# Attention phase of a two-layer gated cross-attention kernel: the weight combinations move from GpSimd to VectorE, three groups of instructions get other places

## The chip, the cores and the metric

The kernel runs on one NeuronCore of a Trainium2 chip. TensorE (PE) multiplies and transposes, VectorE (DVE) and ScalarE (ACT) empty its PSUM banks and do the elementwise work, GpSimd (POOL) does some elementwise work on SBUF, and SyncE (SP) issues most transfers. The metric is the device time of one execution in microseconds. Before the change it is 2092.7 us, the median of three runs (2090.93 to 2093.04).

## The reference

The input x has 8 batches of 512 tokens with 512 features; each batch has a context of 64 tokens. Four residual blocks follow one another, each on a layernorm of x and with a tanh gate:

```python
# 1: linear attention over the context, 16 heads of 32
q = feature_map(xn @ Wq.T); gate = sigmoid(xn @ Wg.T + bg)
k, v = split(ctx @ Wkv.T);  k = feature_map(k)          # feature_map(x) = x+1 if x>0 else exp(x)
attn = (q @ (k.T @ v)) / (q . sum(k) + 1e-6)            # per head
x = x + tanh(g0) * ((attn * gate) @ Wo.T)
# 2: MLP 512 -> 2048 -> 512 with exact gelu
x = x + tanh(h0) * (gelu(xn @ p1.T + b1) @ p2.T + b2)
# 3: masked softmax attention over the context, no weights
x = x + tanh(g1) * softmax(mask(xn @ ctx.T / sqrt(512))) @ ctx
# 4: mixture of 8 dominant experts (router softmax, top 8 of 32, shares merged per group)
x = x + tanh(h1) * sum_g share_g * (silu(xn @ gate_g) * (xn @ up_g)) @ down_g
```

Everything is float32.

## The kernel before, in words

**Phases.** The batches go through three phases, each over all eight: "xa0" (block 1), "ff0" (block 2) and "ff1" (blocks 3 and 4). Between phases x lies in DRAM. Every large matrix product is done with seven instead of eight half-size products (Strassen's scheme in Winograd's form): the operands are first combined by additions. For activations VectorE does this per batch (`token_combinations`, tile S; `combine_inner`, tiles a and s). For weights it is done once per weight.

**Weights of ff0.** p1 and p2 must be combined before ff0 and stored to DRAM again. The generator `build_first` does so in the background of the attention phase, in four rounds i. A round loads a piece of p1 into seven ring tiles (`raw_p1`), combines it with four 128x512 additions (`combining`), stores the seven (`store_up`); loads a piece of p2 into the one build tile (`raw_p2`), combines it with four 128x512 additions, stores three parts of it, combines it a second time with four 128x896 additions in place (`combining_again`), and stores the other parts. Each `yield` ends one call. In the attention loop `tick()` is called after every step of TensorE work and calls the builder at ticks 1 and 3 of each five. All these additions run on GpSimd (`nc.gpsimd`). A second builder, `build_second`, does the like for the weights of ff1 during ff0, on VectorE, through `in_place`.

**Order of the work.** The code is traced in program order, and a planner then orders each engine's queue by its own estimate of when operands are ready. `Ordered` lets the code pin an instruction behind the one traced before it on the same engine: while an engine's name is in the set `in_order`, each of its instructions is pinned; `here(...)` adds engines for a few lines. In the preamble all engines are pinned. In the attention loop SyncE and GpSimd stay pinned, the others not. Each engine then works off its queue strictly in order.

**The preamble.** `keys_values` makes keys, values and, per batch, the key-value products (tile pkv, two PSUM banks per pair of batches), from which VectorE and ScalarE take `summary` and `ksum` (`kept`). Meanwhile batch 0 is normalised and turned.

**The attention loop.** For each batch b there are units of seven products each: `QUp` (queries), `GUp` (gates) and `ODown` (output projection) of the batch before; the last two products of a unit are done after the first of the next. A unit's step n is one product, eight matmuls. Between them stand the denominators of batch b (`denominators`: four matmuls pd, an addition and two reciprocals on VectorE, tile z, a store `over`), the spreading of their values over the heads' partitions by four transfers (`spread`), the gating th = (th + 1) * spread (`gated`, four instructions), the numerators pn on TensorE, and the products a = th * pn (`attended`), which ODown reads. For the last batch there is no next batch's work to hide this behind: `den` is advanced in its own GUp unit from n > 4 on, and from step 4 of ODown of batch 6 on VectorE is pinned, with `gated` after steps 4 and 5.

**Normalisation ahead.** `normed` computes the statistics of the next batch (bn_stats, tile st), rstd on GpSimd, normalises (ScalarE in most of xa0) and transposes. It is advanced by `some(prep)` at given steps; for xa0 and b > 0 first at step 4 of QUp. Its statistics are pinned on VectorE for batch 0 and for later ff0 batches, not for xa0 with b > 0 (line 480).

**Fetches on GpSimd.** The context for block 3 (`c2`, `ctxT` in `cross_attention`), the router weights and the map of expert groups are fetched by GpSimd's queue; in the feed-forward phases GpSimd is not pinned.

Of the kernel before, what the change touches and what calls it, by code (L numbers as in the profile page):

```python
# [30 lines left out]
P = 128  # L31
B, S, D = 8, 512, 512
M = 64
# [35 lines left out]
def flamingo_kernel(  # L69
# [334 lines left out]
    def placed(ph, t):  # L404

        return [t[:, SPLIT_ORDER[ph].index(m)] for m in (1, 5, 2, 3, 6, 7, 4)]

    def build_first():

        def load_up(i):
            t = [ring(f"raw_up{i}_{q}") for q in range(7)]
            raw_p1(t, i)
            return t

        up = load_up(0)
        yield
        for i in range(4):
            for n, _ in enumerate(combining(nc.gpsimd, up)):  # L420
                if n == 2:
                    t = build_tile(f"ff0_down{i}")
                    raw_p2(placed("ff0", t), i)
                yield
            store_up("ff0", i, up)
            for _ in range(2):
                yield
            for n, _ in enumerate(combining(nc.gpsimd, placed("ff0", t))):
                if n % 2:
                    yield  # L430
            if i < 3:
                up = load_up(i + 1)
            yield from combining_again("ff0", i, t, nc.gpsimd, 2)
            yield
        streamed.add("ff0")

    def in_place(steps):

        while True:
            in_order.add("vector")  # L440
            more = next(steps, steps)
            in_order.discard("vector")
            if more is steps:
                return
            yield

    LAND, GAP = 10, 5

# [23 lines left out]
    def normed(ph, b, tag, normed_part=lambda t: None):  # L472

        xb = xs[ph, b]
        xnT = work.tile([P, NC, S], F32, tag="xnT", name=f"xnT_{tag}")
        mv = small.tile([P, NT, 2], F32, tag="mv", name=f"mv_{tag}")
        held = ph == "ff0" and b > 1
        by_scalar = ph == "xa0" and b > 0 or tag == "ff0_0"
        ahead = held or ph == "xa0" and b > 0
        with here(*(["vector"] if held or ph == "xa0" and b == 0 else [])):  # L480
            for t in range(NT):
                st = small.tile([P, 6], F32, tag="st", name=f"st_{tag}_{t}")
                nc.vector.bn_stats(st, xb[:, t, :])
                nc.vector.bn_aggr(mv[:, t, :], st)
        var = small.tile([P, NT], F32, tag="var", name=f"var_{tag}")
        nc.vector.tensor_scalar(var, mv[:, :, 1], LN_EPS, None, ALU.add)  # L486
        rstd = small.tile([P, NT], F32, tag="rstd", name=f"rstd_{tag}")
        if by_scalar:
            shift = small.tile([P, NT], F32, tag="nshift", name=f"nshift_{tag}")
            nc.vector.tensor_scalar(shift, mv[:, :, 0], -1.0, None, ALU.mult)  # L490
        nc.gpsimd.tensor_tensor(rstd, var, neg_half, ALU.pow)  # L491
        if by_scalar:
            nc.gpsimd.tensor_tensor(shift, shift, rstd, ALU.mult)
        if ph in ("xa0", "ff0") or tag.startswith("ff1"):
            yield
        if tag.startswith("ff1"):
            yield
        xn = {}

        def norm(t):  # L500
            xn[t] = work.tile([P, D], F32, tag="xn", name=f"xn_{tag}_{t}")
            with here(*(["vector", "scalar"] if ahead else [])):
                if by_scalar:
                    nc.scalar.activation(
                        xn[t], xb[:, t, :], AF.Identity, bias=shift[:, t : t + 1], scale=rstd[:, t : t + 1]
                    )
                else:
                    nc.vector.tensor_scalar(
                        xn[t], xb[:, t, :], mv[:, t, 0:1], rstd[:, t : t + 1], ALU.subtract, ALU.mult
                    )  # L510

        def turn(t):
            pt = psum(f"pt_{tag}_{t}").rearrange("p (c q) -> p c q", q=P)
            for c in range(NC):
                nc.tensor.transpose(pt[:, c, :], xn[t][:, ts(c, P)], ident)  # L515

            at = t % 2 * 2 + t // 2 if tag.startswith("ff1") else t
            nc.scalar.copy(xnT[:, :, ts(at, P)], pt)

        if ph == "xa0" and b == 0:  # L520
            norm(0)
            norm(1)
            yield
            for t in range(NT):
                turn(t)
                if t + 2 < NT:
                    norm(t + 2)
                yield
            return xnT
        if ahead:  # L530
            norm(0)
            yield
        for t in range(NT):
            if not ahead:
                norm(t)
            elif t + 1 < NT:
                norm(t + 1)
            turn(t)
            normed_part(t)
            yield  # L540
        return xnT
# [109 lines left out]
    def cross_attention(b):  # L651

        xb = xs["ff1", b]
        c2 = hpool.tile([P, D], F32, tag="ctx", name=f"ctxd_{b}", bufs=2)
        for h in range(2):
            nc.gpsimd.dma_start(out=c2[ts(h, M), :], in_=ctx_in[ts(b, M), :])
        maskf = small.tile([P, M], F32, tag="maskf", name=f"maskf_{b}")
        in_order.add("vector")
        nc.vector.tensor_copy(maskf, mask_sb[:, ts(b, M)])
# [4 lines left out]
        nc.vector.reduce_max(gate, maskf, AX.X)  # L664
        nc.vector.tensor_scalar(gate, gate, gate_xa1, None, ALU.mult)
        ctxT = hpool.tile([P, NC, M], F32, tag="ctxdT", name=f"ctxdT_{b}", bufs=2)
        nc.gpsimd.dma_start(out=ctxT, in_=turned[b])
        xnT = yield from normed("ff1", b, f"xa1_{b}")


# [532 lines left out]
    def spread(b):  # L1203

        rows = over[b].rearrange("(c h k) t -> c k h t", c=NC, k=8)
        over[b] = aunits.tile([P, NC, S], F32, tag="over", name=f"spread_{b}")
        for c in range(NC):
            nc.sync.dma_start(out=over[b][ts(c, HD)], in_=rows[c, 0].partition_broadcast(HD))

    def gated(b, th, half):  # L1210

# [15 lines left out]
                )  # L1227
        return pn

    def attended(b, th, pn):  # L1230

        if b < B - 1:
            a = aunits.tile([P, 2, 2, 2, H2], F32, tag="a", name=f"a_{b}")
        else:
            a = work.tile([P, NC, S], F32, tag="xnT", name=f"a_{b}").rearrange(
                "p (r c) (n t) -> p r c n t", c=2, n=2
            )
        for h in range(NC):
            nc.vector.tensor_tensor(
                a[:, :, h // 2, h % 2, :], halves(th[:, h, :]), halves(pn[h]), ALU.mult  # L1240
            )
        for k in ("s1", "s2"):
            inner["x" + k] = aunits.tile([P, 2, H2], F32, tag=k, name=f"{k}_xa0_{b}")
        for r in range(2):
            for c in range(2):
                inner[f"xa{r + 1}{c + 1}"] = a[:, r, c]
        combine_inner(slice(0, 2), "x")
# [92 lines left out]

    def tick():

        if next(ticks) % 5 in (1, 3):
            next(builder, None)

    for b in range(B):
# [19 lines left out]
        for n, (u, m) in enumerate(steps([g])):  # L1366
            u.step(m)
            in_order.discard("tensor")
            tick()
            if n == 1:  # L1370
                if b + 2 < B:
                    load_x("xa0", b + 2)
                elif b + 1 == B:
                    load_x("ff0", 1)
            if b == B - 1 and n > 4:
                next(den, None)
            if n == 3 or n > 3 and not done:
                some(prep)
# [7 lines left out]
            spread(b)  # L1386
            pn = numerators(b, q.q)
        for n, (u, m) in enumerate(steps([ODown(done[0])] if done else [])):
            if b == B - 1 and n == 4:
                in_order.add("vector")  # L1390
            u.step(m)
            in_order.discard("tensor")
            if b < B - 1:
                next(den, None)
                if n == 6:
                    spread(b)
            elif n in (4, 5):
                gated(b, g.th, n - 4)
            elif n == 6:
                attended(b, g.th, pn)  # L1400
            if n in ((0, 1, 3, 5) if b < B - 1 else (6,)):
                some(prep)
            tick()
        in_order.discard("vector")
        for _ in prep:
            pass
        done = b, q.q, g.th
# [65 lines left out]
        next(loads)  # L1473
    hpool = stack(tc.tile_pool(name="inner", bufs=1, reuse_waits="tile"))
    router_sb = hpool.tile([P, NC, E], F32, tag="router_w", name="router_sb")
    nc.gpsimd.dma_start(out=router_sb, in_=router.rearrange("(c p) e -> p c e", p=P))

    of_group = hpool.tile([P, G, E], F32, tag="of_group", name="of_group")
    mg_i = hpool.tile([P, E], I32, tag="mg_i", name="mg_i")
    nc.gpsimd.dma_start(out=mg_i, in_=mg.rearrange("e o -> o e").partition_broadcast(P))  # L1480
    mg_f = hpool.tile([P, E], F32, tag="mg_f", name="mg_f")

    def groups():
        nc.vector.tensor_copy(mg_f, mg_i)
# [12 lines left out]
    for u, m, n in plan:  # L1497
# [29 lines left out]
            next(builder, None)  # L1527
        if n + 1 == 3 * B:
            continue
        if n == B + 2 and k == 10:  # L1530
            groups()
        if k == 20 and n + 2 < 3 * B:
# [61 lines left out]
```

## Time and profile before

| | |
|---|---|
| Median of the runs | 2092.7 us |
| Profiled execution, own time | 2091.8 us |
| Its span | 2090.0 us |
| Instructions in it | 35123 |
| Preamble, to the first q product | 0 to 61.2 us |
| Attention loop, to the first ff0 product | 61.2 to 412.9 us |
| ff0 and ff1 | 412.9 to 2090.0 us |
| VectorE busy, 61.2 to 350.0 | 208.6 of 288.8 us |
| GpSimd busy, 61.2 to 350.0 | 82.7 of 288.8 us |
| DMA moved | 484.67 MB |

A row of the profile names the line of the kernel, the engine, the operation and the tiles, output first ("ksum<-pkv,heads"). Line 60 is the wrapper `Ordered`: it stands for every pinned instruction, so those are told apart by tile. "xN" is a count, and in square brackets is the engine's idle time just before, with what ended it. PEclk is the share of full speed that TensorE was granted. Stretches of time count from the start of the span.

### The profile page before, as it was taken

What the parts mean: (1) busy time and instruction counts of PE and PEld (TensorE: products, weight loads), DVE (VectorE), ACT (ScalarE), POOL (GpSimd) and SP (SyncE); (2) the same over time, 40 slices, a digit from 0 to 9 for tenths busy, and PEclk for the clock granted to TensorE, in tenths of its full rate; (3) what the DMA queues carried; (4) which work ended last, traced back from release to release, by engine and by line L of the source; (5) the groups of instructions that cost most, each with busy time, mean ns of one, the idle gap of its engine ahead of it and who ended that gap; (6) DMA issues with size and microseconds to landing.
All of it is one profiled execution on the core that took longest, in us unless ns stands there. A gap on an engine that the chain in (4) does not pass through costs nothing.

```text
span 2090.0 us, 35123 instructions
## 1 busy us (share of the span) xinstructions
PE 2050.6 (98%) x12796; PEld 1820.7 (87%) x12796; DVE 1488.7 (71%) x2941; ACT 629.4 (30%) x1294; POOL 172.0 (8%) x172
## 2 busy tenths in 40 slices
PE   7999999899999999999999999999999999999998
PEld 4777877699999998999989989898989889898988
DVE  3577777748667585868767687777777676876758
ACT  2544343242323324242334222312222222223121
POOL 3233132100000000000000010100000010100000
PEclk8999999999999999999999999999999999999999
DMA  6355655498889887889887858586776858585865
GB/s 197 122 177 153 206 168 173 135 303 293 285 264 298 286 291 255 282 279 286 273 255 244 278 172 284 185 267 210 243 225 210 267 173 290 159 287 158 271 202 170
DMA packets 304171, 484.67 MB, mean 232 GB/s; under 512 B 36992, under 2 KB 103712, under 8 KB 299904
## 3 DMA queue, kind: packets, MB, share of 16 engines
q1 hardware_dynamic: 296560, 455.65, 69.0%
q10 hardware_dynamic: 5856, 23.20, 3.0%
q0 software_dynamic: 1584, 3.57, 0.6%
q8 instruction: 103, 1.69, 0.3%
q14 instruction: 68, 0.56, 0.1%
HBM read 413.04 MB, written 69.27 MB: 231 GB/s over the span
## 4 chain that ended last, share of the span: by engine, by line
PE 90%; DVE 5%; DMA 2%; ACT 1%; SPq 1%; issue 1%; POOL 0%; ACTq 0%; DVEq 0%; POOLq 0%
PE x_ff L855 26%; PE w_ff L855 13%; PE x_ff_down L1050 13%; PE w_ff_down L1050 8%; PE z_ff L855 7%; PE z_ff_down L1050 4%; PE v_ff_down L1050 4%; PE x_xa_down L971 2%; PE x_q L855 2%; PE pt_ff L515 1%; PE pt_xa L515 1%; PE x_g L855 1%; PE w_xa_down L971 1%; SPq L60 1%; PE pst L675 1%; PE pr L720 1%
## 5 line engine op out<-in xcount | busy, mean ns | idle before, releaser
L855 PE MATMUL x_ff<-S_ff,w_ff 128*128 128x256 f32 x1280 | 304.2, 380 | 0.0
L855 PE MATMUL w_ff<-S_ff,w_ff 128*128 128x256 f32 x1280 | 303.4, 380 | 0.0
L855 PE MATMUL x_ff<-xnT_ff,w_ff 128*128 128x256 f32 x1280 | 294.5, 379 | 0.0
L867 ACT COPY u_ff<-x_ff 128x512 f32<-128x512 f32 x240 | 140.1, 584 | 475.0 <-PE x_ff L855 447.3
L855 PEld LDWEIGHTS x_ff<-S_ff,w_ff 128*128 128x128 f32 x1280 | 240.5, 190 | 40.2 <-issue 5.7
L855 PEld LDWEIGHTS w_ff<-S_ff,w_ff 128*128 128x128 f32 x1280 | 239.0, 190 | 32.2 <-issue 1.4
L855 PEld LDWEIGHTS x_ff<-xnT_ff,w_ff 128*128 128x128 f32 x1280 | 237.8, 190 | 30.8 <-ACT a_ff L915 0.4
L1050 PE MATMUL x_ff_down<-w_ff_down,split_ff_down 128*128 128x128 f32 x1344 | 157.9, 275 | 0.0
L1050 PEld LDWEIGHTS x_ff_down<-w_ff_down,split_ff_down 128*128 128x128 f32 x1344 | 153.9, 192 | 0.0
L855 PE MATMUL z_ff<-xnT_ff,w_ff 128*128 128x256 f32 x640 | 151.4, 379 | 0.0
L1064 DVE TENSOR_TENSOR part_ff_down<-part_ff_down 128x128 f32<-128x128 f32 x315 | 85.6, 289 | 67.4 <-ACT part_ff_down L1077 59.7
L855 PEld LDWEIGHTS z_ff<-xnT_ff,w_ff 128*128 128x128 f32 x640 | 119.8, 190 | 15.3
L1050 PE MATMUL w_ff_down<-w_ff_down,split_ff_down 128*128 128x128 f32 x896 | 105.3, 275 | 0.0
L1050 PEld LDWEIGHTS w_ff_down<-w_ff_down,split_ff_down 128*128 128x128 f32 x896 | 102.6, 192 | 0.0
L910 DVE TENSOR_TENSOR a_ff<-w_ff,u_ff 128x512 f32<-128x512 f32 x64 | 43.9, 686 | 74.5 <-ACT u_ff L867 74.4
L915 ACT ACTIVATE a_ff<-a_ff,b_sb 128x256 f32<-128x256 f32 x128 | 58.1, 501 | 94.6 <-DVE a_ff L910 94.6
L491 POOL TENSOR_TENSOR rstd_ff<-var_ff,neg_half 128x4 f32<-128x4 f32 x15 | 15.9, 1057 | 818.7 <-DVE var_ff L486 818.7
L938 DVE SCALAR_TENSOR_TENSOR g_ff<-th_ff,x_ff 128x512 f32<-128x512 f32 x48 | 32.8, 684 | 70.3 <-ACT th_ff L937 70.3
L1050 PE MATMUL w_ff_down<-w_ff_down,s_ff 128*128 128x128 f32 x672 | 81.5, 275 | 0.0
L1050 PE MATMUL x_ff_down<-w_ff_down,a_ff 128*128 128x128 f32 x672 | 80.4, 275 | 0.0
L1050 PEld LDWEIGHTS w_ff_down<-w_ff_down,s_ff 128*128 128x128 f32 x672 | 79.4, 192 | 0.8
L1050 PEld LDWEIGHTS x_ff_down<-w_ff_down,a_ff 128*128 128x128 f32 x672 | 78.4, 192 | 0.5
(269 smaller groups left out, 3450.7 us busy)
## 6 DMA issues: line engine op xcount, KB each, us to landing
w_ff_down<-stream_ff SPq DMA_DIRECT2D x680, 256.0 KB
w_ff<-ff_up SPq DMA_DIRECT2D x560, 256.0 KB
stream_ff<-build_ff_down SPq DMA_DIRECT2D x49, 448.0 KB
x_ff<-x_ff SPq DMA_DIRECT2D x16, 1024.0 KB
share<-shares SPq DMA_DIRECT2D x64, 256.0 KB
ff_up<-build_ff_up SPq DMA_DIRECT2D x42, 256.0 KB
spread<-over SPq DMA_DIRECT2D x32, 256.0 KB
x_ff<-x_xa ACTq DMA_DIRECT2D x8, 1024.0 KB
```

The source lines that it names most:

```text
L60: made = f(*args, **kw)
L515: nc.tensor.transpose(pt[:, c, :], xn[t][:, ts(c, P)], ident)
L675: nc.tensor.matmul(pst[ts(r, M), :], lhsT=ctxT[:, c, :], rhs=xnT[:, c, :].rearrange("p (u r q) -> p r u q", u=2, r=2)[:, r], start=c == 0, ...
L720: nc.tensor.matmul(pr[t], lhsT=eT[half, t // 2, :], rhs=c2[half, :], start=True, stop=True)
L855: nc.tensor.matmul(p[:, n, :], lhsT=w[:, c, ts(n, P)], rhs=moving, **self.mark(m, 2 * n + c),)
L867: nc.scalar.copy(self.s[m], p)
L910: nc.vector.tensor_tensor(h, p, s, ALU.add)
L915: nc.scalar.activation(h[:, n, :], p[:, n, :], AF.Gelu, bias=b1_sb[:, f : f + 1])
L938: nc.vector.scalar_tensor_tensor(g, th, 1.0, p, ALU.add, ALU.mult)
L971: nc.tensor.matmul(p[:, t, :], lhsT=a[:, k, ts(t, P)], rhs=w[k // 2][:, k % 2, :], **self.mark(m, 2 * k + t),)
L1050: nc.tensor.matmul(p[bank][:, place, :], lhsT=operand[k][:, c, :], rhs=w[at // 4][:, ts(at % 4, P)], start=bank not in opened, stop=True, ...
L1064: return lambda: nc.vector.tensor_tensor(m(k), m(k), m(by), ALU.add)
```

## The change

It has five parts.

1. `build_first` calls `combining` and `combining_again` on `nc.vector` instead of `nc.gpsimd`, through `in_place`, which pins each addition behind the VectorE instruction traced before it. One addition is now done per call also in the first combination of p2, and there are two more empty calls at the start and one more after `store_up`: 75 calls in place of 61. `tick()` makes a call at every second tick.
2. In `normed` the statistics of all xa0 batches are pinned.
3. For the last batch `spread` sends the denominators in two halves of two heads each (eight transfers of half the size), `gated` is called by `attended`, each half ahead of its two products, and VectorE is no longer pinned in ODown's last steps.
4. The last batch's denominators begin one step earlier (n > 3).
5. The context fetches of `cross_attention` are pinned on GpSimd at their place in the program, and the fetches of the router and of the groups' map move from the start of ff0 to its second batch (`load_router`).

```diff
-    def build_first():
...
-            for n, _ in enumerate(combining(nc.gpsimd, up)):
...
-            store_up("ff0", i, up)
-            for _ in range(2):
-                yield
-            for n, _ in enumerate(combining(nc.gpsimd, placed("ff0", t))):
-                if n % 2:
-                    yield
-            if i < 3:
-                up = load_up(i + 1)
-            yield from combining_again("ff0", i, t, nc.gpsimd, 2)
...
+    def build_first():
...
+        up = load_up(0)
+        for _ in range(3):
+            yield
+        for i in range(4):
+            for n, _ in enumerate(in_place(combining(nc.vector, up))):
+                if n == 2:
+                    t = build_tile(f"ff0_down{i}")
+                    raw_p2(placed("ff0", t), i)
+                yield
+            store_up("ff0", i, up)
+            for _ in range(3):
+                yield
+            yield from in_place(combining(nc.vector, placed("ff0", t)))
+            if i < 3:
+                up = load_up(i + 1)
+            yield from in_place(combining_again("ff0", i, t, nc.vector, 2))
+            yield
+        streamed.add("ff0")
...
-        with here(*(["vector"] if held or ph == "xa0" and b == 0 else [])):
+        with here(*(["vector"] if held or ph == "xa0" else [])):
...
-        for h in range(2):
-            nc.gpsimd.dma_start(out=c2[ts(h, M), :], in_=ctx_in[ts(b, M), :])
+        with here("gpsimd"):
+            for h in range(2):
+                nc.gpsimd.dma_start(out=c2[ts(h, M), :], in_=ctx_in[ts(b, M), :])
...
-        nc.gpsimd.dma_start(out=ctxT, in_=turned[b])
+        with here("gpsimd"):
+            nc.gpsimd.dma_start(out=ctxT, in_=turned[b])
...
-        for c in range(NC):
-            nc.sync.dma_start(out=over[b][ts(c, HD)], in_=rows[c, 0].partition_broadcast(HD))
+        for h in [slice(0, 2), slice(2, 4)] if b == B - 1 else [slice(0, 4)]:
+            for c in range(NC):
+                nc.sync.dma_start(out=over[b][ts(c, HD), h], in_=rows[c, 0, h].partition_broadcast(HD))
...
-    def attended(b, th, pn):
+    def attended(b, th, pn, ahead=lambda b, th, half: None):
...
         for h in range(NC):
+            if h % 2 == 0:
+                ahead(b, th, h // 2)
...
-        if next(ticks) % 5 in (1, 3):
+        if next(ticks) % 2:
             next(builder, None)
...
-            if b == B - 1 and n > 4:
+            if b == B - 1 and n > 3:
                 next(den, None)
...
-            if b == B - 1 and n == 4:
-                in_order.add("vector")
             u.step(m)
...
-            elif n in (4, 5):
-                gated(b, g.th, n - 4)
             elif n == 6:
-                attended(b, g.th, pn)
+                attended(b, g.th, pn, gated)
...
-        in_order.discard("vector")
...
-    nc.gpsimd.dma_start(out=router_sb, in_=router.rearrange("(c p) e -> p c e", p=P))
...
-    nc.gpsimd.dma_start(out=mg_i, in_=mg.rearrange("e o -> o e").partition_broadcast(P))
...
+    def load_router():
+        with here("gpsimd"):
+            nc.gpsimd.dma_start(out=router_sb, in_=router.rearrange("(c p) e -> p c e", p=P))
+            nc.gpsimd.dma_start(out=mg_i, in_=mg.rearrange("e o -> o e").partition_broadcast(P))
...
+        if n == B + 1 and k == 10:
+            load_router()
```

More of the change, by code (lines that the diff above doesn't have):

```diff
@@ L406, in placed @@
         return [t[:, SPLIT_ORDER[ph].index(m)] for m in (1, 5, 2, 3, 6, 7, 4)]
-    def build_first():
[L412 to L417, printed above, removed]
-        yield
-        for i in range(4):
-            for n, _ in enumerate(combining(nc.gpsimd, up)):
-                if n == 2:
-                    t = build_tile(f"ff0_down{i}")
-                    raw_p2(placed("ff0", t), i)
-                yield
-            store_up("ff0", i, up)
-            for _ in range(2):
-                yield
-            for n, _ in enumerate(combining(nc.gpsimd, placed("ff0", t))):
-                if n % 2:
-                    yield
-            if i < 3:
-                up = load_up(i + 1)
-            yield from combining_again("ff0", i, t, nc.gpsimd, 2)
-            yield
-        streamed.add("ff0")
     def in_place(steps):
@@ L445, in in_place, with load_up @@
             yield
+    def build_first():
+        def load_up(i):
+            t = [ring(f"raw_up{i}_{q}") for q in range(7)]
+            raw_p1(t, i)
+            return t
+        up = load_up(0)
[16 more added lines that the diff above has]
+        streamed.add("ff0")
     LAND, GAP = 10, 5
```

## The prediction

> **What bounds the kernel now.** I read the totals, the busy time by stage, TensorE's waits, and the order of work around the longest of them.
>
> ```profile
> span 2090.0 us, 35123 instructions
> ...
> PE 2050.6 (98%) x12796; PEld 1820.7 (87%) x12796; DVE 1488.7 (71%) x2941; ACT 629.4 (30%) x1294; POOL 172.0 (8%) x172
> ```
>
> TensorE is the bound as a whole: 2090.0 - 2050.6 = 39.4 us idle. The stages say where (span; busy us and instructions of each engine; granted clock; DMA share; GB/s):
>
> ```profile
> core 0: us, PE busy (x) PEld busy (x) DVE busy (x) ACT busy (x) POOL busy (x), PEclk, DMA share, GB/s
> 27.69:39.87 12.18, 0.01 (x1) 0.04 (x1) 1.04 (x3) 4.24 (x12) 7.52 (x6) 0.62 0.71 183
> 39.87:61.22 21.35, 19.77 (x81) 10.97 (x81) 11.98 (x36) 6.33 (x18) 7.39 (x8) 0.82 0.41 122
> 61.22:350.00 288.78, 279.86 (x1502) 229.60 (x1503) 208.61 (x303) 120.40 (x219) 82.74 (x58) 0.99 0.53 161
> 350.00:412.87 62.87, 55.74 (x309) 44.47 (x308) 48.64 (x85) 18.43 (x33) 7.21 (x11) 0.92 0.53 155
> ```
>
> The last 1677 us (both feed-forward phases) are 99.5% busy at full clock, apart from the tail after the last matmul. What an edit of the attention phase can win lies before 412.87: 12.2 + 1.6 + 8.9 + 7.1 us idle in these four rows, and cold clock beside it. TensorE's waits, longest first (total, times, longest):
>
> ```profile
> PE pkv L60 <- DVE ksum L60: 12.2, 1, 12.2
> PE x_xa_down L971 <- DVE x_xa L60: 6.8, 1, 6.8
> PE x_g L855 <- ACT u_g L867: 6.1, 4, 2.2
> ```
>
> The first, in order of time:
>
> ```profile
> 27.92 1.35 SPq L60 DMA_DIRECT2D x_xa<-in_x  x1
> 38.83 0.69 DVE L483 BATCH_NORM_STATS2 st_xa<-x_xa 128x6 f32<-128x512 f32 x1 [15.72 <-DMA x_xa<-in_x]
> 39.44 0.28 DVE L60 TENSOR_TENSOR ksum<-pkv,heads 128x128 f32<-128x128 f32 x1
> 39.87 0.60 PE L60 MATMUL pkv<-v,k 64*128 64x160 f32 x1 [12.18 <-DVE ksum L60]
> ```
>
> Batch 1's statistics (L483, not pinned for b > 0) stand in VectorE's queue ahead of the key sums, though the code needs them only in the loop. Their x lands at 38.8, VectorE stands still for 15.7 us, and the banks of the key products stay full. The third wait is made of gaps like this one:
>
> ```profile
> 310.80 8.15 POOL L60 TENSOR_TENSOR build_ff_down<-build_ff_down 128x512 f32<-128x512 f32 x5 [21.62 <-DMA build_ff_down<-in_p]
> 315.21 1.80 DVE L894 TENSOR_TENSOR s_xa<-a 128x512 f32<-128x512 f32 x1
> 317.05 2.45 DVE L895 TENSOR_TENSOR s_xa<-s_xa,a 128x512 f32<-128x512 f32 x1
> 319.42 0.68 DVE L896 TENSOR_TENSOR a<-a 128x512 f32<-128x512 f32 x1
> 323.25 0.92 PE L855 MATMUL x_g<-S_xa,w_g 128*128 128x256 f32 x3 [2.20 <-ACT u_g L867]
> ```
>
> While POOL combines weights, VectorE's adds take 1.8 and 2.45 us instead of 0.68; the evacuations behind them come late. And the last row's end:
>
> ```profile
> 376.48 1.75 SPq L60 DMA_DIRECT2D spread<-over  x4
> 387.03 2.50 DVE L60 SCALAR_TENSOR_TENSOR th<-th,spread 128x512 f32<-128x512 f32 x4 [5.60 <-DMA spread<-over]
> 389.44 0.75 DVE L60 SCALAR_TENSOR_TENSOR x_xa<-x_xa_down,gates_half,x_xa 128x512 f32<-128x512 f32 x1
> 390.24 2.08 PE L971 MATMUL x_xa_down<-w_o,a 128*128 128x256 f32 x4 [6.75 <-DVE x_xa L60]
> ```
>
> Gating is pinned ahead of two evacuations and waits for the spread; TensorE stops at 383.49.
>
> **What the Trainium skill says.** SBUF — State Buffer, "Who interferes with whom": a VectorE instruction with two SBUF inputs contends with a GpSimd instruction that reads SBUF, and whoever comes second fully blocks. The trace agrees: among VectorE's groups from 61 to 413 us, s_xa<-s_xa,a (L895) has a mean of 1463 ns, but a<-th,pn and qs_q<-w_q,u_q, with one input in PSUM, stay at 679 and 686. TensorE: Matmul & The Clock Gate, "What's actually happening": an idle window of about 3.4 us halves the clock. Here the granted clock is 0.62 and 0.82 around the 12.2 us stall.
>
> **The change part by part.**
>
> *Statistics pinned (start).* x1's statistics go behind the VectorE work traced before them, in the first batch's q unit. Gone: 12.18 us of stall, 0.53 us of a second wait at 40.73 behind the same statistics, and the cold clock, 0.18 x 21.35 = 3.8 us in the second row. Less 0.2 for overlap: **-16.3 us**. What is late next? Redoing the start from the rows' durations: key sums at 23.3 to 25.1, w_q's four adds from 30.2 (two may meet POOL's w_g adds from 32.0, 1.3 us each), the next key sums by 35.3; TensorE wants them only at 27.7 + 1.4 + 3.7 + 3.6 = 36.4. The q unit then starts at about 45 instead of 61.2. x1 landed at 38.8, before the statistics' new place (about 52). If the cover of 1.1 us fails, 1 to 2 us are lost.
>
> *Combining on VectorE (loop).* POOL loses 32 adds of 128x512 and 16 of 128x896 (22.2 + 21.5 + 35.7 = 79.4 us). VectorE prices: later builds do both shapes on it, at 0.684 us and, at the most, 1.092: 32 x 0.684 + 16 x 1.09 = 39.3 us. Against that the contention goes. In the groups with two SBUF inputs, over 0.685 (0.692 for q) apiece: q 2.9, L895 5.4, L896 4.0, L894 3.0, L634 2.5, L635 1.6, L637 1.2, L636 1.0, together 21.6 us. Net +17.7 us of VectorE in some 330 us: from about 280 of 352 (80%) to 298 of 330 (90%) by durations; less in truth, since back-to-back adds start 0.60 us apart (398.74, 399.34). So it still fits under TensorE. The six larger gaps of the loop (0.60, 0.44, 1.42, 1.21, 0.52, and 2.21 with 2.20) all follow adds stretched by POOL: 8.6 us, and 3.4 us at half clock after the last, 1.7. Bounds of this part: -10.3 (all recovered) to +8 (each of seven blocks loses about 1 us to adds standing before an evacuation, over what they lose now). I take **-6**, since new adds are single and 0.7 to 1.1 us long, where the stretched ones cost 5 us in a row.
>
> Pace: the loop has 12 + 7 x 21 = 159 ticks. The old builder needs 61 calls and gets 64; the new needs 75 and gets 79. It still ends in the loop, hidden by it. Behind a waiting add stands all of VectorE: evacuations, features, then TensorE. The add at risk is the second of the second combining, which overwrites what its three stores read. It comes three calls, six steps of 1.73 us, 10.4 us after their issue; on POOL the adds began 3.3 to 8.0 us after the last store's issue, which itself takes some 3 us. So a wait of 0 to 1 us a build. The p1 and p2 loads have 14 and 10 steps or more; SP runs ahead of them.
>
> *Halves at the end.* Four more issues on SP, 4 x 0.43 = 1.7 us, ahead only of the w_ff prefetches, which TensorE needs 30 us later. Spread's issue to landing is 387.03 - 376.48 = 10.55 us; of that 1.75 is issue and about 2 is start (over took 2.06 from issue to release), so half of the remaining 6.8 lands the first half at an estimated 1.75 + 2 + 3.4 = 7.1, so the first half's gating ends 3.4 us sooner, and its two products follow at once instead of behind all four gatings and two evacuations. First product pair ready: 374.42 + 2.06 + 7.1 + 2.5 = 386.1 against about 392.2; the second, landing no sooner than now, about 390.5 against 393.4. The evacuations leave the pinned order and run early. The denominators are begun one step earlier, but q ends at 367.1 and TensorE already waits 0.29 us for it, so that gives at most 0.5 and may move a wait. Output projection earlier by 3 to 6: **-5**, bounds -9 (gap and cold clock gone) to +1 (q's wait moved onto TensorE, nothing won).
>
> *Fetches moved.* Router, groups and context fetches leave POOL's queue at 376.9 to 381.5 (some 4 us of issue) for the ff phases. They landed in 4.5 to 9.4 us; the first use is a block (94 us) later for the router, some six preparation steps for the context: nothing, hidden by matmuls; if groups were tried before landing, VectorE would lose up to 9 us once, with 30% idle there.
>
> Sum: -16.3 - 6 - 5 = -27.3. The profiled execution took 2091.8, so 2064.5; the median of the runs, 2092.7, lies 0.9 above it: **2065.4 us**, own range 2056 to 2073.
>
> **Rivals.**
> 1. *VectorE becomes the loop's bound.* For: 90% by durations. Against: 0.60 us spacing, and a builder add at most every other step. Then the loop gives +8 instead of -6: 2079.
> 2. *The start's stall stays with another head,* another early instruction taking the statistics' place: -11 only: 2082. Against: nothing else on VectorE there reads a late transfer.
> 3. *VectorE waits for the builder's stores* (the slower one). POOL waited 95.3 us in four waits on them, harmlessly; on VectorE, TensorE has some 2 us of cover (it stopped 2.06 us after VectorE did at 381.43). It decides from 4 x (W - 2.1) = 27.3, W = 8.9 us a build; at the full 23.8 it costs 87: 2152. Against: most of POOL's wait was before the stores were issued.
>
> **How the numbers follow.** Likeliest 0.62, rival 1 0.19, rival 2 0.06, rival 3 0.10, nothing 0.03. The range 2055 to 2083 leaves out rival 3 and the edges. Within 0.2% (4 us) is about what a measurement can't tell from no change; faster is 0.62 + 0.19 + 0.06 = 0.87, same 0.03, slower 0.10.
>
> **What would show it.** No wait of pkv for ksum, and full clock from 28 to 48 us; L894 to L896 at 0.69 us; POOL nearly empty after 45 us; TensorE's loop gaps under 5 us; the last gap near 2 to 4 us; first feed-forward matmul near 386 instead of 412.9. Wrong: VectorE waits on stream_ff or raw_up transfers, x_g waits grown, or a wait of pd for q above 3 us.

## The result and the profile after

The changed kernel takes 2057.0 us, median of six runs (2056.34 to 2058.08), against 2092.87 us (2090.93 to 2095.74): 0.9829 of the time before, 95% interval 0.9816 to 0.9842. Its profiled execution took 2056.86 us. The page of the changed kernel, its totals:

```profile
span 2055.1 us, 35088 instructions
...
PE 2040.4 (99%) x12796; PEld 1814.5 (88%) x12796; DVE 1501.5 (73%) x2989; ACT 629.3 (31%) x1294; POOL 97.7 (5%) x124
```

TensorE's idle time fell from 39.4 us to 14.7; GpSimd went from 172.0 busy us to 97.7, VectorE rose by 12.8 only. By stage (length; busy us and instructions of PE, PEld, DVE, ACT, POOL; granted clock; DMA share; GB/s):

```profile
27.69:45.00 17.31, 16.26 (x83) 9.16 (x84) 9.66 (x24) 10.62 (x30) 10.59 (x8) 1.00 0.65 165
45.00:330.00 285.00, 283.13 (x1560) 233.51 (x1559) 224.96 (x364) 124.30 (x224) 13.48 (x14) 1.00 0.58 175
330.00:380.00 50.00, 48.23 (x258) 38.19 (x257) 46.54 (x81) 15.32 (x29) 2.21 (x3) 1.00 0.47 157
```

The stall of 12.18 us after 27.69 is gone, TensorE stands still for 1.9 us in 285 of the loop, and the clock is full in all three rows. Where the stall was, the key sums now end ahead of the key-value products that need their banks:

```profile
35.23 0.29 DVE L60 TENSOR_TENSOR ksum<-pkv,heads 128x128 f32<-128x128 f32 x1
...
35.91 1.36 PE L60 MATMUL pkv<-v,k 64*128 64x160 f32 x16
```

What TensorE still waits for in the attention phase (total, times, longest):

```profile
PE x_g L856 <- ACT u_g L868: 1.1, 3, 0.4
PE x_q L856 <- DVE ksum L60: 0.8, 1, 0.8
...
PE pd L1191 <- DVE q L621: 0.7, 1, 0.7
```

The wait of pkv for ksum (12.2 us) has no line any more, that of x_xa_down for x_xa (6.8) neither, and the gate unit's wait for u_g went from 6.1 to 1.1. VectorE's groups in the loop (count, then busy us and mean ns of one, then idle time just before them):

```profile
L60 DVE TENSOR_TENSOR build_ff_down<-build_ff_down 128x896 f32<-128x896 f32 x16 | 17.2, 1076 | 0.9 <-DMA stream_ff<-build_ff_down 0.9
...
L60 DVE TENSOR_TENSOR raw_up<-raw_up,raw_up 128x512 f32<-128x512 f32 x16 | 10.9, 684 | 0.1
...
L896 DVE TENSOR_TENSOR s_xa<-s_xa,a 128x512 f32<-128x512 f32 x8 | 5.5, 683 | 0.0
```

The builder's additions now stand here, the 128x512 ones at 684 ns like VectorE's other additions of that size; they waited for their stores 0.9 us in all. Among VectorE's own additions for the output projection, s_xa<-s_xa,a (L895 before) takes 683 ns where its mean was 1463. The end, in order of time:

```profile
349.65 4.54 SPq L60 DMA_DIRECT2D spread<-over  x8
...
355.18 1.29 DVE L1215 SCALAR_TENSOR_TENSOR th<-th,spread 128x512 f32<-128x512 f32 x2
...
356.39 1.28 DVE L1243 TENSOR_TENSOR a<-th,pn 128x512 f32<-128x512 f32 x2
...
361.85 1.28 DVE L1215 SCALAR_TENSOR_TENSOR th<-th,spread 128x512 f32<-128x512 f32 x2
```

Neither gating has a wait in front of it.

**Where the time went.** Three marks split every run: the first q product, the first z_q product of the last batch, and the first feed-forward product (x_ff). "Start" is the time up to the first mark, "loop" the first to the second, "end" the second to the third, "rest" from the third to the last matmul's end; all in us, from one profiled execution.

| kernel | median of runs | start | loop | end | rest |
|---|---|---|---|---|---|
| before | 2092.87 | 61.22 | 285.97 | 65.52 | 1670.48 |
| after | 2057.0 | 44.39 | 275.55 | 58.13 | 1670.44 |
| difference | -35.9 | -16.8 | -10.4 | -7.4 | 0.0 |

### The profile page after: what moved, and what is told of

Its sections match the earlier page's. It is cut to its first block, busy times and chain, and to the rows that moved or that the text cites. A ratio compares the mean times of both kernels' runs of the same rounds, so it can differ in the third digit from the quotient of the medians.

```text
span 2055.1 us, 35088 instructions
## 1 busy us (share of the span) xinstructions
PE 2040.4 (99%) x12796; PEld 1814.5 (88%) x12796; DVE 1501.5 (73%) x2989; ACT 629.3 (31%) x1294; POOL 97.7 (5%) x124
## 5 line engine op out<-in xcount | busy, mean ns | idle before, releaser
L949 DVE TENSOR_TENSOR up_ff<-w_ff,u_ff 128x512 f32<-128x512 f32 x96 | 65.6, 684 | 17.7 <-ACT u_ff L868 17.7
```

The costliest lines, as they stand in the source:

```text
L949: nc.vector.tensor_tensor(u, p, s, ALU.add)
```

## Experiments

The table gathers all runs; the sections below take them by question. "Ratio" is against the kernel before, measured beside each run, with its 95% interval. The kernel before had medians of 2092.87 to 2094.56 us beside the different runs, so a difference of a run from the changed kernel's 2057.0 of a microsecond or so is not told from none.

| run | what it is | median us | ratio | start | loop | end |
|---|---|---|---|---|---|---|
| e1_stats_free | after, part 2 undone | 2073.65 | 0.9913 (0.9886 to 0.9940) | 60.65 | 275.11 | 58.12 |
| e2_stats_only | before, part 2 alone | 2088.81 | 0.9974 (0.9968 to 0.9981) | 44.13 | 302.00 | 66.13 |
| e12_first_pin | before, pinned for batches 0 and 1 only | 2077.35 | 0.9916 (0.9901 to 0.9931) | 44.29 | 288.32 | 65.18 |
| e3_builder_pool | after, part 1 undone | 2084.81 | 0.9958 (0.9947 to 0.9968) | 44.26 | 299.61 | 61.35 |
| e7_pool_adds | after, idle additions on GpSimd | 2072.88 | 0.9902 (0.9879 to 0.9925) | 43.68 | 292.01 | 58.13 |
| e8_pool_sets | after, idle fills on GpSimd | 2056.39 | 0.9821 (0.9798 to 0.9844) | 44.51 | 275.55 | 58.12 |
| e9_vector_twice | after, idle additions on VectorE | 2071.13 | 0.9892 (0.9869 to 0.9915) | 43.76 | 285.72 | 62.82 |
| e10_no_gap | after, no pause before the second combination | 2064.58 | 0.9861 (0.9838 to 0.9885) | 43.93 | 280.96 | 60.25 |
| e4_end_old | after, parts 3 and 4 undone | 2063.79 | 0.9857 (0.9832 to 0.9882) | 44.25 | 276.03 | 65.49 |
| e6_whole | after, spread whole, rest of the end kept | 2060.36 | 0.9842 (0.9829 to 0.9855) | 44.59 | 275.55 | 61.44 |
| e5_den_late | after, part 4 undone | 2056.73 | 0.9826 (0.9813 to 0.9838) | 43.89 | 276.08 | 57.99 |
| e11_fetch_old | after, part 5 undone | 2057.04 | 0.9828 (0.9815 to 0.9841) | 44.31 | 275.54 | 58.12 |

### The statistics: taken out of after, put alone into before

e1_stats_free is the changed kernel without part 2 (the diff), e2_stats_only the kernel before with part 2 alone (the diff the other way round):

```diff
-        with here(*(["vector"] if held or ph == "xa0" else [])):
+        with here(*(["vector"] if held or ph == "xa0" and b == 0 else [])):
```

> The changed kernel with batch 1's and later attention statistics left unpinned, as before. My theory (the pin alone ends the stall in the preamble): the 12 us wait of pkv for ksum comes back and the first q product moves from 44.4 back to about 61 us; time about 2057 + 16.8 = 2074 us. Rival (the statistics only stood early because the builder's work was on GpSimd, so that VectorE looked free): the order on VectorE stays good without the pin and the time stays at 2057.

> The kernel before with the statistics of all attention batches pinned, and nothing else. My theory: the start's gain alone, 16.3 us as forecast or 16.8 as the two traces have it: about 2076 us, the loop's gaps unchanged. Rival (the statistics in their later place meet a VectorE slowed by GpSimd, and the loop loses some of it): 2079 to 2085.

Left out of the changed kernel, the pin costs 16.65 us, all of it at the start. The order of time in e1_stats_free:

```profile
39.54 0.69 DVE L482 BATCH_NORM_STATS2 st_xa<-x_xa 128x6 f32<-128x512 f32 x1 [15.92 <-DMA x_xa<-in_x]
...
40.57 0.87 PE L60 MATMUL pkv<-v,k 64*128 64x160 f32 x2 [13.27 <-DVE ksum L60]
```

The same stall behind the same instruction: the mechanism of the prediction holds. Put alone into the kernel before, however, the pin won the 17 us at the start and lost 16 in the loop of the profiled execution; by the medians, which give 5.0 us in all, some 12 were lost. The rival had a smaller loss (3 to 9 us), and by another way. The order of time in e2_stats_only, at the worst of its new gaps:

```profile
309.54 1.01 POOL L60 TENSOR_TENSOR rstd_xa<-var_xa,neg_half 128x4 f32<-128x4 f32 x1 [33.59 <-ACT qs_q L1158]
...
313.68 8.88 POOL L60 TENSOR_TENSOR build_ff_down<-build_ff_down 128x512 f32<-128x512 f32 x5
314.19 1.75 DVE L895 TENSOR_TENSOR s_xa<-s_xa,a 128x512 f32<-128x512 f32 x1
315.86 1.75 DVE L896 TENSOR_TENSOR a<-a 128x512 f32<-128x512 f32 x1
...
318.24 0.63 ACT L620 ACTIVATE fe_q<-qs_q 128x512 f32<-128x512 f32 x1 [7.36 <-DVE qs_q L1156]
...
320.76 1.65 PE L855 MATMUL x_g<-S_xa,w_g 128*128 128x256 f32 x3 [6.00 <-ACT u_g L867]
```

GpSimd is pinned, and rstd, which reads the statistics, stands in its queue ahead of the builder's additions. With the statistics at their traced place rstd comes late: GpSimd idles 33.6 us with additions pent up behind it (20.98, 34.83, 26.89 and 28.92 before the four rstd that precede this one; 0.6 to 10 us before the same five in the kernel before). They then run in one block, just where VectorE has its burst of additions for the output projection. The means of L895 and L896 rise from 1463 and 1257 ns to 1696 and 1678. Behind them stands the evacuation qs_q; ScalarE waits 7.36 us for it before it can go on to copy u_g, and that copy ends TensorE's gap. In the loop TensorE's idle time rises from 8.9 us to 17.8, and the time at half clock from 3.4 us to 20.5, which costs about as much again.

To test that reading, e12_first_pin pins in the kernel before only what the start needs.

```diff
-        with here(*(["vector"] if held or ph == "xa0" and b == 0 else [])):
+        with here(*(["vector"] if held or ph == "xa0" and b < 2 else [])):
```

> The kernel before with the statistics pinned for batches 0 and 1 only, so that the start is as in the changed kernel and the later batches stand as before. Theory: the loop's loss in the run with all statistics pinned (16 us) comes from the pinned statistics of batches 2 to 7 moving rstd, and the combining pinned behind it on GpSimd, into the burst of VectorE's adds; then the start keeps its 17 us, the loop stays at 286 us, 2076 us. Rival: the loss comes with the earlier start itself (another phase between builder, transfers and loop); then the loop takes 300 us or so and the time is near 2089.

The start keeps its 17 us, the loop takes 288.3 us, and the time is 2077.35 us: the earlier start by itself costs the loop some 2 us (and the six runs of this kernel lie 7.6 us apart); the rest of the loss comes with the later batches' pins. In its order of time, the same rstd, the last batch's, comes 39 us sooner, after a short wait and with two additions behind it:

```profile
270.18 1.01 POOL L60 TENSOR_TENSOR rstd_xa<-var_xa,neg_half 128x4 f32<-128x4 f32 x1 [7.31 <-DVE var_xa L486]
...
271.41 2.62 POOL L60 TENSOR_TENSOR raw_up<-raw_up,raw_up 128x512 f32<-128x512 f32 x2
```

### The combining: back on GpSimd

e3_builder_pool is the changed kernel with the old `build_first`, its engine and its pace.

```diff
-            for n, _ in enumerate(in_place(combining(nc.vector, up))):
+            for n, _ in enumerate(combining(nc.gpsimd, up)):
...
-        if next(ticks) % 2:
+        if next(ticks) % 5 in (1, 3):
```

> The changed kernel with the weight combinations back on GpSimd, at the old pace; statistics pinned, halves and fetches as in the change. My theory (contention stretches VectorE's adds and so makes the loop's gaps): adds L895 to L897 back at 1.1 to 1.5 us on average, six or seven gaps of 0.4 to 2.2 us in the loop, 8 to 11 us lost: 2065 to 2068 us. Rival (the loop's gain came from the statistics' place or the pace): no more than 3 us lost, 2057 to 2060.

It costs 27.8 us, 24.1 of it in the loop and 3.2 at the end: two and a half times the theory's 8 to 11, which had reckoned with the loop of the kernel before. TensorE's waits for u_g are those of e2_stats_only; the first line is e2_stats_only's, the second e3_builder_pool's:

```profile
PE x_g L855 <- ACT u_g L867: 16.4, 5, 6.0
```

```profile
PE x_g L857 <- ACT u_g L869: 16.4, 5, 6.0
```

The four long gaps agree to a hundredth (2.56, 4.38, 2.92 and 6.01 us against 2.57, 4.38, 2.93 and 6.00). So part 1 is worth 24 us in a loop with pinned statistics, and 11 in one without (before against e1_stats_free, which has parts 3 to 5 too: 285.97 and 275.11). Parts 1 and 2 are not additive: part 2 alone gives 5.0 us (2093.77 in the runs beside it, to 2088.81), all the others without it 20.1, together 36. Engine and pace of the builder were changed together; no run has the one without the other.

### Is it the port, or GpSimd's queue?

Three kernels put idle work beside the changed one's builder. Nothing is left out of the computation; a ring of temporary tiles has seven instead of eight. The idle work of e7_pool_adds is 64 additions on GpSimd that read SBUF, of e8_pool_sets 256 fills there that read nothing, of e9_vector_twice 64 additions on VectorE, pinned.

```diff
+                for _ in range(times):
+                    nc.gpsimd.tensor_tensor(dummy, dummy, dummy, ALU.subtract)   # e7_pool_adds
...
+                    for _ in range(4):
+                        nc.gpsimd.memset(dummy, 0.0)   # e8_pool_sets
...
+                    in_order.add("vector")
+                    nc.vector.tensor_tensor(dummy, dummy, dummy, ALU.subtract)   # e9_vector_twice
+                    in_order.discard("vector")
```

> The changed kernel, the builder on VectorE, and beside each of its additions idle additions of 128x512 on GpSimd, on a tile that nobody reads (64 in all, some 81 us at 1.27 us; the ring of temporary tiles has seven buffers instead of eight to make room, and the mask is fetched as in the change). Theory (GpSimd reading SBUF holds up VectorE's additions with two SBUF inputs): s_xa, a and the builder's own additions stretch to 1.1 to 2 us, the loop's gaps come back; the additions run in bursts behind each rstd, so at least what e3 lost: 2080 to 2100 us. Rival (e3 lost its time to the builder's place in GpSimd's queue and its waits, not to the port): within 3 us of the change, 2057 to 2060.

> The same with four fills of 128x512 on GpSimd in place of each idle addition: as much work in GpSimd's queue, but it reads no SBUF. Theory: additions on VectorE stay near 0.68 us and the time near the change's, 2057 to 2061. Rival (any work on GpSimd, or the later rstd behind it, costs): as e7.

> The changed kernel with each of the builder's additions doubled on VectorE by idle ones of 128x512 on a tile that nobody reads (64 more, 38 us at the 0.60 us from start to start; seven temporary buffers). It asks how near VectorE is to being the loop's bound, my first rival. Theory (in the change VectorE is idle for 60 of the 285 us from 45 to 330, so doubling still fits): 2 to 8 us lost, 2059 to 2065. Rival (it was at 90% and bounds): 25 us or more lost, above 2080.

Groups of VectorE and of GpSimd in e7_pool_adds:

```profile
L1168 DVE TENSOR_TENSOR qs_q<-w_q,u_q 128x512 f32<-128x512 f32 x16 | 10.9, 684 | 6.7 <-ACT u_q L879 4.1 <-PE w_q L867 2.6
...
L908 DVE TENSOR_TENSOR a<-a 128x512 f32<-128x512 f32 x7 | 9.0, 1282 | 0.0
L60 POOL TENSOR_TENSOR dummy<-dummy 128x512 f32<-128x512 f32 x64 | 83.8, 1310 | 4.5
```

The same in e8_pool_sets:

```profile
L909 DVE TENSOR_TENSOR a<-a 128x512 f32<-128x512 f32 x8 | 5.5, 684 | 0.0
L60 POOL MEMSET dummy<- 128x512 f32 x256 | 134.5, 525 | 14.3
```

With 83.8 us of reading additions on GpSimd, a<-a takes 1282 ns instead of 684 and the run is 15.9 us longer, all of it in the loop, but less than its forecast of 23 at least; qs_q<-w_q,u_q, with one input in PSUM, stays at 684. With 134.5 us of fills in the same queue, and the same shorter ring, nothing moves (2056.39). So it is not the length of GpSimd's queue but what its instructions read, as the Trainium skill says (SBUF — State Buffer, "Who interferes with whom": not with one that only writes SBUF). The two engines' additions then end in turn: in e2_stats_only GpSimd's at 315.39, VectorE's at 315.94, GpSimd's at 317.06, VectorE's at 317.61. Each of VectorE's takes 1.75 us and ends 0.55 us after one of GpSimd's, as if one ran while the other stood still. The idle additions stand at other places than the old builder's; how much of e3_builder_pool's larger loss (24.1 us in the loop against 16.5) is place and how much pace, no run shows.

e9_vector_twice asks how near VectorE is to being the bound. Its loop, with the columns of the stages above:

```profile
45.00:330.00 285.00, 277.05 (x1487) 226.69 (x1486) 248.64 (x408) 120.62 (x218) 13.24 (x14) 0.99 0.56 166
```

VectorE goes from 224.96 to 248.64 us of 285 (79% to 87%), and 14.1 us are lost for 43.7 us of additions, a third of a microsecond for each, where 2 to 8 had been expected; 10.2 of them are lost in the loop, 4.7 at the end, and the start is 0.6 shorter. VectorE does not have to be full for its additions to cost. Whether the load costs or the pinned place ahead of evacuations, this run doesn't tell; the next one shows that place alone can cost.

### Waiting for the stores

e10_no_gap lets the second combination of p2 follow its stores without calls between (the two calls go elsewhere).

```diff
-            for _ in range(3):
+            for _ in range(5):
...
-            yield from in_place(combining_again("ff0", i, t, nc.vector, 2))
+            yield from in_place(combining_again("ff0", i, t, nc.vector, 0))
```

> The changed kernel with the two empty calls between the builder's stores and its second combination moved ahead of the first combination of p2: the same pace, but the addition that overwrites what a store reads comes two steps (3.5 us) after the stores' issue instead of six (10.4). Theory (stores need some 6 to 11 us from the first issue): VectorE waits 3 to 7 us on a store in each of the four rounds, and TensorE, with 2 us of cover, loses 1 to 5 us each: 2061 to 2075. Rival (the planner puts other work ahead of the addition, or the cover is larger): 2057 to 2059.

It costs 7.6 us. That lies in the theory's range by luck, since it does not come from what was expected: VectorE waited for stores 2.8 us in all, in two waits. The rest goes with other gaps, among them one behind which the clock halves (TensorE's waits):

```profile
PE x_g L856 <- ACT u_g L868: 4.0, 3, 1.7
PE pd L1191 <- DVE q L621: 3.2, 2, 2.7
```

That the additions now stand elsewhere in VectorE's queue, ahead of evacuations, is the likely reason; no run isolates it, so it stays open.

### The end, piece by piece

e4_end_old undoes parts 3 and 4; e6_whole only sends the spread whole again; e5_den_late only begins the denominators at n > 4 again.

```diff
-        for h in [slice(0, 2), slice(2, 4)] if b == B - 1 else [slice(0, 4)]:
+        for h in [slice(0, 4)]:   # e4_end_old, e6_whole
...
-            if b == B - 1 and n > 3:
+            if b == B - 1 and n > 4:   # e4_end_old, e5_den_late
...
+            if b == B - 1 and n == 4:   # these and the next: e4_end_old
+                in_order.add("vector")
...
+            elif n in (4, 5):
+                gated(b, g.th, n - 4)
             elif n == 6:
-                attended(b, g.th, pn, gated)
+                attended(b, g.th, pn)
...
+        in_order.discard("vector")
```

> The changed kernel with the last batch's end as before: whole spread, gating pinned after steps 4 and 5, denominators one step later. My theory: the gap of some 6 us and half clock before the last output projection come back, 7.4 us lost: about 2064 us. Rival (the gap was caused by the slowed VectorE ahead of it and closes without the new end): 2057 to 2059.

> The changed kernel with the denominators spread whole (four transfers) instead of in halves; the gating stays in attended, VectorE unpinned, denominators early. Theory: the halves carry the gain; the spread's issue to landing returns to some 10.5 us against 7.6 for the first half, so the first product pair comes 3 us later, a gap of 2 to 4 us opens before the last output projection, with a cold clock after it: 2059 to 2062. Rival: the gain came from taking the two evacuations out of the pinned order; then 2057, no gap.

> The changed kernel with part 4 undone: the last row's denominators begin one step later again. Theory (as the prediction has it): q ends where it did, so TensorE's wait of pd for q (0.69 us) goes, but the denominators' chain starts a step of about 1.7 us later and ends later; net within 1 us of 2057. Rival: the earlier start carried part of the 7.4 us at the end; then the gap before the last output projection comes back by 1 to 2 us, 2058 to 2059.

e4_end_old brings back a gap of 5.9 us (357.23 to 363.14) and half clock to 369.1 (TensorE's waits):

```profile
PE x_xa_down L972 <- DVE x_xa L60: 5.9, 1, 5.9
```

The end takes 65.49, as before. e6_whole takes 61.44 and e5_den_late 57.99. So of the 7.4 us at the end, 4.1 (65.5 to 61.4) come with the gating and the evacuations out of their pinned order, 3.3 with the halves after that, and nothing with the earlier denominators, which only move the wait of pd for q. No run has the halves with the old pinned order, so the division holds for this order of steps alone. Theory and rival of e6_whole had each given the gain to one side; it is divided. In e6_whole, in order of time:

```profile
349.84 1.75 SPq L60 DMA_DIRECT2D spread<-over  x4
...
360.39 0.75 DVE L988 SCALAR_TENSOR_TENSOR x_xa<-x_xa_down,gates_half,x_xa 128x512 f32<-128x512 f32 x1 [1.30 <-PE x_xa_down L972]
...
361.06 1.28 DVE L1215 SCALAR_TENSOR_TENSOR th<-th,spread 128x512 f32<-128x512 f32 x2
```

Gating starts 11.2 us after the issue instead of 5.5, but other evacuations stand ahead of it with no pin, and TensorE's gaps there are four of 0.8 to 1.1 us, after which the clock stays full. The completion records of the transfers in the two traces divide the 5.7 us: the last of the whole spread landed 9.7 us after the first issue, the last of the first half 5.4 (the expectation's 7.6 was too late), so 4.3 us are the landing. The other 1.4 are the planner's order: VectorE idles and then evacuates x_xa (360.39) although the values have landed.

### The fetches

e11_fetch_old puts the router, map and context fetches back (part 5).

```diff
-        with here("gpsimd"):   # c2, ctxT, router and map: not pinned
+        if True:
...
+    load_router()
...
-        if n == B + 1 and k == 10:
-            load_router()
```

> The changed kernel with part 5 undone: router and groups' map fetched at the start of ff0, context fetches not pinned. Theory: nothing on the path that sets the end reads them early; 2057 within 1 us, and the two feed-forward phases stay at 1670.4 us from first to last product. Rival: their queue on GpSimd or the DMA engines they share with the last row's spread matter; then the spread lands later or the phases grow, 2058 to 2062.

2057.04 us: part 5 does nothing that can be measured, in the attention phase or after it.

## Why the prediction was right, and where its sizes were off

Its sum was -27.3 us against the profiled execution; the spans differ by 34.9. The time lies in its range, near the low end, 8.4 us under its number: all three terms were put too small, and no error made up for another.

- **Start, -16.3: measured -16.8**, and 16.65 by undoing it. The wait removed, the second wait and the cold clock are the whole of it; the q unit starts at 44.4 (about 45 was worked out). The next key sums ended at 35.5 and pkv followed at 35.9 without a wait for them, so the cover was 0.4 us where 1.1 had been worked out. Rival 2 falls.
- **Loop, -6: measured -10.4**, at the bound it gave for everything recovered (-10.3). The term mis-sized is the 4.3 us taken off for additions standing ahead of evacuations: idle time of 1.9 us and no half clock are what is left. That it meets the bound so closely is chance: TensorE's idle time in the loop fell by 7.1 us (8.9 to 1.9) and the half clock explains 1.7; the last 1.7 us, by which the same 1488 matmuls took less, was in no term, and no run explains it. The builder's price was right (39.0 us against 39.3).
- **End, -5: measured -7.4.** The chain was right and the first half came sooner than the estimated 7.1 us (within 5.5), but the sum credited the halves with the gain; 4.1 of it came with the evacuations' and the gating's freedom, named there in one sentence without a price. The last gap, put at 2 to 4 us, is 0.6. "At most 0.5" for the earlier denominators holds (0).
- **Fetches, 0: measured 0**, and the rest stays at 1670.4.
- **Rival 1, VectorE as the bound.** Its 90% was right, and didn't bind. It adds up the durations of VectorE's instructions: 279.8 us of 352 before (80%) and 300.1 of 335 after (90%, from 45 to 380). Additions that follow one another overlap in the record, 0.60 us from start to start at 0.68 us each, so the stage rows, which count a moment once, have less: 208.6 + 48.6 = 257 of 352 (73%) and 225.0 + 46.5 = 271.5 of 335 (81%). The danger is real, though: at 87% by the rows e9_vector_twice loses 14 us, by load or by place.
- **Rival 3, waits on stores.** "A wait of 0 to 1 us a build" holds: 0.9 us in all four. Even without the pauses it is 2.8, far under the 8.9 a build from which it would decide.
- **What the working didn't see.** It priced each part against the kernel before and added up. Part 2 in the kernel before would have cost 12 to 16 us in the loop through rstd's place on GpSimd; that it doesn't is owed to part 1, which leaves no additions behind rstd. The working asked what stands behind a waiting VectorE instruction, and not what stands behind the GpSimd instruction that reads the moved result. Here the omission cost nothing, since both parts came together; that was luck, not foresight.

## What to carry to other kernels

When an instruction is pinned or moved, follow its result to the queue of the engine that reads it, and list what is pinned behind that reader: there the time may be lost that was won at the first place. Here GpSimd's work with SBUF inputs cost time wherever it met VectorE's two-input SBUF work that TensorE waited for; work there that only wrote cost nothing. Parts that touch the same engine are to be tried alone and together, since here 5 and 20 us made 36. And the length of TensorE's gaps is not all that counts for its clock: their place does too, as the next section shows.

## What the runs showed of the hardware that was not expected

- 256 fills on GpSimd, 134.5 us, left VectorE's additions at 684 ns; 64 additions, 83.8 us, brought one group to 1282.
- Gaps of 2 to 3 us in TensorE's work halve the clock in some cases only, and the traces show which. The clock changes at ticks 3.41 us apart: before 420 us, the fourteen traces have 20 stretches at half clock, of 3.41, 6.83, 10.24, 13.65 or 17.07 us, and those of one trace start whole numbers of ticks apart (before: at 30.65, 324.19 and 385.63, 86 and 18 ticks). By the matmul records from 15 to 420 us, the clock halved after stretches between two ticks in which TensorE had been idle for 1.90 to 3.41 us in all, and after none with less; it stayed full after all others, of which the longest idle time is 1.94. It came back to full only after a stretch with at most 0.29 us idle; with 0.37 and more it stayed at half.
- So in the kernel before the gap of 2.20 us at 321, which lies whole between two ticks (320.78 and 324.19), was followed by 3.4 us at half clock, and that of 2.21 at 278, which a tick at 279.82 divides into 1.68 and 0.54, by none; in e12_first_pin 2.72 us of one of 2.89 lie between two ticks, and 1.65 of one of 2.61, which the clock outlasted. The Trainium skill (TensorE: Matmul & The Clock Gate, "What's actually happening") has an idle window of about 3.4 us, free-running. The window is in these traces; 1.9 us of idle time in it sufficed here.
- VectorE cost TensorE time before it was full: when additions on it raised its busy share of the loop from 79% to 87%, 0.32 us were lost for each microsecond of them.
